# When VectorE reads a product that TensorE makes behind two heads' convolutions: its steps ordered behind the masks, and one product of routed weights placed behind shared unit 1

## The chip, the cores and the metric

The kernel runs on one core of a Trainium2 chip. A core has five engines with a queue of instructions each: TensorE (PE, matrix products; its weight loads are listed as PEld), VectorE (DVE), ScalarE (ACT), GpSimdE (POOL) and SyncE (SP), which mostly starts DMAs. They meet through semaphores: an instruction at the head of its queue waits until what it needs has been signalled, and everything behind it on the same engine waits too. The metric is the device time of one execution in microseconds (us).

## The reference: what is computed

`x` has 128 sequences of 32 heads (rows) with 512 positions each. Cut to what matters here:

```
K[h, l]   = 2 Re sum_n Ct[h,n] exp(dtA[h,n] l)              # a kernel of 512 taps per head
y[b,h]    = (causal convolution of x[b,h] with K[h] + D[h] x[b,h]) * (l < length[b])
scores    = sigmoid(y @ gate_w.T) + bias                    # 4096 rows y[b,h], 16 experts
the 4 best experts of each row, their scores scaled to sum 1
out       = x + sum over the 4 experts of w * ((silu(y Wg) * (y Wu)) Wd)
              + (silu(y Sg) * (y Su)) Sd                    # an expert that all rows share
```

All matrix products that carry y are in float32.

## The kernel before, in words

The work has three stages, and TensorE's order in each is written by hand.

**Convolutions.** The heads are done one at a time for heads 0 and 1 and then in pairs: (2,3), (4,5) up to (30,31). `convolve` (L593) multiplies the transposed input `xt` with `strip`, a 128 x 512 tile per head in which row p is the head's kernel shifted by p, into two PSUM tiles `py0` and `py1` (L599). VectorE then multiplies each with the mask `within` of the sequence lengths and writes `yb` (L617, "the mask"). One pair uses both PSUM tiles, so the next pair can only overwrite each once its mask is done. After the convolutions of a pair, `behind_head` (L943) puts other products in TensorE's order, first for the even head and then for the odd one: `turn_y` (L619, product L623) transposes the masked head before, which ScalarE copies to `yT` (L624); `gates` (L635, product L644) and `sums` (L658, product L661) make the gate's products into `parts` and `pg`; `kernels` (L379, product L407) makes the kernels of further heads into `pk`; the generator `ranks` (L502) sorts the sequences by length in small products (`by_rank_ps` L513, `k_u_ps` L533, `row_ps` L552); `weights_out` (L719, product L724) brings the chosen weights back to the order of rows.

The kernels of heads are made in six chunks of 4 to 8 heads. VectorE, ScalarE and GpSimdE make a chunk's exponentials and angles (`waves`, L303, held behind an earlier chunk's last step by `behind`), then the factors `gg_r`, `gg_i` (L398 to L403); TensorE multiplies them into `pk`; VectorE adds the skip term (`krow`, L415); SyncE writes the rows to memory (L422) and reads them back as `strip` (L433), one strip of 1 MB per four heads, in two buffers. Chunks 1 to 5 have their product behind heads 0, 3, 8, 14 and 20.

`route` (L669) chooses the experts of eight heads. It begins on VectorE with L683, which reads `pg`, and goes on through some 35 steps of 128 columns (a sigmoid in exp_parts L262 to L278, eight maxima L691, scans) to the weights `cw` (L716).

TensorE's order is fixed. VectorE's is not: the framework's scheduler sorts its instructions by the times that it assumes for them, and VectorE then executes them strictly in that order. The pairs of masks, the steps of the waves, and the steps that read `pk`, `by_rank_ps`, `k_u_ps`, `row_ps` and `pg` stand in one queue.

**Shared units.** Eight units of 512 rows go through the shared expert (`up` L1046, product L1052; `down` L1062, product L1067) in `unit_step` (L1094). Between them the generator `slots` (L737) makes the lists of routed tiles. `route` of the last eight heads stands behind the first quarter of unit 0, and two products of routed weights, of head blocks 2 and 3, behind unit 0:

```
        if u == 0:
            weights_out(NB // RB - 2)
            weights_out(NB // RB - 1)
```

**Routed tiles.** 134 tiles of 128 rows are gathered (L1017), transposed (L1147), multiplied with their expert's weights (L1179, L1205), and added to the output in memory (L1215).

Of the kernel before, what the change touches and what calls it, by code (L numbers as in the profile page):

```python
# [33 lines left out]
ALU = mybir.AluOpType  # L34
# [5 lines left out]
B, H, L, N = 128, 32, 512, 64  # L40
E, TOPK, I = 16, 4, 256
# [38 lines left out]
def ssm_moe_kernel(  # L80
# [15 lines left out]
    nc = tc.nc  # L96
# [61 lines left out]
    def dep(of, on, why):  # L158
        tc.add_manual_dep(of.ins, on.ins.name, SYNC, reason=why)
# [296 lines left out]

    chunk_last = {0: chunk0}

    def behind(op, c0=CHUNKS[2][0]):


        own = [c for c, _ in CHUNKS].index(c0)
        dep(op, chunk_last[CHUNKS[own - 1 if own > 2 else 0][0]], "later in VectorE's order")
# [38 lines left out]
    def ranks():  # L502

        to_rank_h = const.tile([P, P], F16, tag="to_rank_h", name="to_rank_h")
        last_chunk = chunk_last[max(chunk_last)]

        def later(op):
            dep(op, last_chunk, "later in VectorE's order")

        later(nc.vector.tensor_copy(to_rank_h, to_rank))  # L510

        by_rank_ps = ps_m.tile([P, 2], F32, tag="m", name="by_rank_ps")
        nc.tensor.matmul(by_rank_ps, lhsT=to_rank_h, rhs=num_len, start=True, stop=True)  # L513
        by_rank = const.tile([P, 2], F32, tag="by_rank", name="by_rank")
        nc.vector.tensor_copy(by_rank, by_rank_ps)
        yield


        reach = const.tile([P, KT], BF16, tag="reach", name="reach")
        later(nc.vector.memset(reach, 1.0))  # L520
        for n in range(1, KT):
            nc.vector.tensor_scalar(
                reach[:, n : n + 1], by_rank[:, 1:2], float(n * P), None, ALU.is_gt
            )

        unit = const.tile([P, NU], BF16, tag="unit", name="unit")
        later(nc.vector.tensor_scalar(unit, upos, 0.0, None, ALU.is_equal))
        reach_sum = const.tile([P, 1], F32, tag="reach_sum", name="reach_sum")
        nc.vector.tensor_reduce(reach_sum, reach, AX.X, ALU.add)
        reach_b = const.tile([P, 1], BF16, tag="reach_b", name="reach_b")  # L530
        nc.vector.tensor_copy(reach_b, reach_sum)
        k_u_ps = ps_m.tile([1, NU], F32, tag="m", name="k_u_ps")
        nc.tensor.matmul(k_u_ps, lhsT=reach_b, rhs=unit, start=True, stop=True)  # L533
        yield
        k_u = const.tile([1, NU], I32, tag="k_u", name="k_u")
        nc.vector.tensor_copy(k_u, k_u_ps)


        div = const.tile([P, 2], F32, tag="div", name="div")
        mod = const.tile([P, 1], F32, tag="mod", name="mod")  # L540
        later(floor_div(div[:, 0:1], rank, UB))
        later(floor_div(div[:, 1:2], ppos, UB))
        nc.vector.scalar_tensor_tensor(mod, div[:, 0:1], -float(UB), rank, ALU.mult, ALU.add)
        same_mod = const.tile([P, P], F16, tag="same_mod", name="same_mod")
        nc.vector.tensor_scalar(same_mod, pmod, mod, None, ALU.is_equal)
        row_u = const.tile([P, NU], F16, tag="row_u", name="row_u")
        nc.vector.tensor_scalar(
            row_u, cpos[:, :NU], div[:, 0:1], ppos, ALU.is_equal, ALU.mult
        )
        yield  # L550
        row_ps = ps_m.tile([P, NU], F32, tag="m", name="row_ps")
        nc.tensor.matmul(row_ps, lhsT=same_mod, rhs=row_u, start=True, stop=True)  # L552
        part = const.tile([P, TU // P], F32, tag="part", name="part")
        nc.vector.tensor_scalar(
            part, cpos[:, : TU // P], float(P // UB), div[:, 1:2], ALU.mult, ALU.add
        )
        unit_rows = const.tile([P, NU, TU // P], I32, tag="unit_rows", name="unit_rows")
        nc.vector.scalar_tensor_tensor(
            unit_rows,
            row_ps.unsqueeze(2).to_broadcast([P, NU, TU // P]),  # L560
            float(H),
            part.unsqueeze(1).to_broadcast([P, NU, TU // P]),
            ALU.mult,
            ALU.add,
        )
        of_ranks.update(by_rank=by_rank, reach=reach, k_u=k_u, unit_rows=unit_rows)


# [6 lines left out]
    within = const.tile([P, L], F32, tag="within", name="within")  # L575
# [14 lines left out]
    pys = [ps_g.tile([P, L], F32, tag="g", name=f"py{i}") for i in range(2)]  # L590
    skip = {}

    def convolve(tb, qs, xt, yb):  # L593
        def products(n):
            c0 = n * TS
            for q in qs:
                for jt in range(KT):

                    nc.tensor.matmul(  # L599
                        pys[q % 2][:, c0 : L - jt * P],  # L600
                        lhsT=xt[:, jt, q, :],
                        rhs=strip[tb][:, q, jt * P + c0 :],
                        start=(jt == 0),
                        stop=(jt == KT - 1 or L - (jt + 1) * P <= c0),
                    )
                    if L - (jt + 1) * P <= c0:
                        break

        if len(qs) == 1:
            products(0)  # L610
        else:

            if not skip:
                skip[0] = nc.tensor.value_load(skips[0:1, 0:1], min_val=0, max_val=SKIPS - 1)
            by_number(skip[0], 0, SKIPS - 1, products)
        for q in qs:
            nc.vector.tensor_mul(yb[:, q, :L], pys[q % 2], within)  # L617

    def turn_y(h, yb):  # L619
        q = h % HB  # L620
# [12 lines left out]
    pgs, cws, by_head, parts_last = {}, {}, {}, []  # L633
# [35 lines left out]
    def route(rb):  # L669
        nh = RB * HB  # L670
        hs = slice(rb * nh, (rb + 1) * nh)

        def stile(name, shape=(nh, E)):
            return sp.tile([P, *shape], F32, tag=name, name=f"{name}{rb}")

        def flat(t):
            return t.rearrange("p h e -> p (h e)")

        def over_e(t):
            return t.to_broadcast([P, nh, E])  # L680

        s, neg = stile("s"), stile("neg", (nh * E,))
        nc.vector.tensor_scalar(neg, pgs[rb][:, : nh * E], -1.0, None, ALU.mult)  # L683
        exp_into(neg, neg, f"sig{rb}", sp)
        nc.vector.tensor_scalar(neg, neg, 1.0, None, ALU.add)
        nc.vector.reciprocal(flat(s), neg)
        nc.vector.tensor_add(s, s, bias_b.unsqueeze(1).to_broadcast([P, nh, E]))

        top = stile("top", (nh, 8))
        for n in range(nh):  # L690
            nc.vector.max(top[:, n, :], s[:, n, :])  # L691
        last = top[:, :, TOPK - 1 : TOPK]
        above, same, nth, free = stile("above"), stile("same"), stile("nth"), stile("free", (nh, 1))
        nc.vector.tensor_tensor(above, s, over_e(last), ALU.is_gt)
        nc.vector.tensor_tensor(same, s, over_e(last), ALU.is_equal)
        heads_run = run_e[:, :nh, :]
        nc.vector.tensor_tensor_scan(
            flat(nth), flat(heads_run), flat(same), 0.0, ALU.mult, ALU.add
        )
        nc.vector.tensor_reduce(free[:, :, 0], above, AX.X, ALU.add)  # L700
        nc.vector.tensor_scalar(free, free, -1.0, float(TOPK), ALU.mult, ALU.add)
        nc.vector.tensor_tensor(nth, nth, over_e(free), ALU.is_le)
        nc.vector.tensor_mul(same, same, nth)
        nc.vector.tensor_add(above, above, same)
        nc.vector.tensor_copy(sel[:, :, hs].rearrange("p e h -> p h e"), above)
        nc.vector.tensor_tensor_scan(
            flat(nth), flat(heads_run), flat(above), 0.0, ALU.mult, ALU.add
        )
        nc.vector.tensor_mul(choice[:, hs, :], nth, above)
        nc.vector.tensor_mul(s, s, above)  # L710
        tot = stile("tot", (nh, 1))
        nc.vector.tensor_reduce(tot[:, :, 0], s, AX.X, ALU.add)
        nc.vector.tensor_scalar(tot, tot, 1e-20, None, ALU.add)
        nc.vector.reciprocal(free, tot)
        cw = stile("cw")
        nc.vector.tensor_mul(cw, s, over_e(free))  # L716
        cws[rb] = cw
# [225 lines left out]
    def behind_head(h):  # L943
# [4 lines left out]
        if h in kernels_at:  # L948
            c = kernels_at[h]
            chunk_last[c[0]] = kernels(*c, *made_waves[c])  # L950

        if strips[-1] in (tb, tb + 1) and strips[-1] < NB and strips[-1] * HB in kd_of:
            kernel_strip(strips[-1])
# [140 lines left out]
    def unit_step(u):  # L1094
# [15 lines left out]
                    next(making, None)  # L1110
        if u == 0:
            weights_out(NB // RB - 2)
            weights_out(NB // RB - 1)
        for q in range(TU // P):
            if u > 0:
# [227 lines left out]
```

## Time and profile before

| | us |
|---|---|
| median of 3 runs | 930.07 (929.57 to 930.26) |
| the profiled execution | 929.21 |
| its span, first to last instruction | 927.5 |
| TensorE busy | 877.9 |
| VectorE busy | 413.8 |
| convolutions, 22.5 to 135.5 us of the span | 113.0, TensorE busy 99.2, VectorE 78.2 |
| shared units, 135.5 to 279 us | 143.5, TensorE busy 140.7 |
| routed tiles, 279 us to the end | 648.5, TensorE busy 632.0 |

Two views answer most questions about such a kernel. The list of waits says which line of an engine waited for which line of another, for how long in total, how often, and the longest. The timeline lists one engine's instructions in order: start and length in us, line, output and inputs, shape, and, in square brackets, idle time before it and what ended that. Float32 products are issued in two halves, so that eight records are one set of four products. PEclk is the clock granted to TensorE as a share of full speed.

### The profile page before, as it was taken

Reading aid. Unit: us, or ns where it says so; the run is one execution under the profiler, and the core shown is the slowest. Engines: PE = TensorE matmul, PEld = TensorE weight load, DVE = VectorE, ACT = ScalarE, POOL = GpSimd, SP = SyncE. Lnnn points to the kernel's source line nnn. Section 1 sums busy time; section 2 is a strip of 40 time slices with the busy share of each in tenths; the row PEclk is TensorE's granted clock in tenths of the full one; section 3 lists DMA queues with packets and bytes.
Section 4 is the critical chain, followed back from the end, with each engine's and each line's share of the span. In section 5 each row is a group of like instructions: output and inputs, shape, how many; then the busy total and the mean of one; then the engine's idle time right before and its main releaser. Section 6 shows DMA issues by size and latency. Waiting matters only on the chain. (4 is left out here: it accounts for less than half of the span.)

```text
span 927.5 us, 14675 instructions
## 1 busy us (share of the span) xinstructions
PE 877.9 (95%) x2976; PEld 447.9 (48%) x2976; DVE 413.8 (45%) x1488; ACT 189.5 (20%) x379; POOL 420.7 (45%) x372
## 2 busy tenths in 40 slices
PE   2878899999999999999999999999999999999994
PEld 1656664444444444444444444444444444544441
DVE  8857655677841233423343334333433233343332
ACT  1221221111222112212221122211221112122211
POOL 1210010223456455645564556545655545556554
PEclk9998999999999999999999999999999999999998
DMA  5675659496869766776678567756766556677575
GB/s 204 198 232 173 222 175 333 56 317 120 151 153 206 163 115 118 141 174 105 115 137 187 102 111 136 127 103 110 132 113 114 102 100 109 114 126 138 106 127 102
DMA packets 54710, 136.03 MB, mean 147 GB/s; under 512 B 12432, under 2 KB 12592, under 8 KB 50992
## 3 DMA queue, kind: packets, MB, share of 16 engines
q0 software_dynamic: 36256, 89.77, 53.3%
q1 hardware_dynamic: 14096, 36.15, 11.4%
q10 hardware_dynamic: 4224, 8.39, 2.4%
q8 instruction: 76, 1.25, 0.5%
q14 instruction: 58, 0.48, 0.2%
HBM read 288.08 MB, written 60.64 MB: 376 GB/s over the span
## 5 line engine op out<-in xcount | busy, mean ns | idle before, releaser
L1179 PE MATMUL g<-store,yt 128*128 x742 | 343.1, 596 | 2.1 <-issue 1.3
L1215 POOL DMA_INDIRECT out<-ob,put x134 | 212.2, 1584 | 234.5 <-DVE junk L1154 189.8
L1205 PE MATMUL o<-store,zT 128*128 x536 | 252.0, 592 | 0.0
L1191 DVE SCALAR_TENSOR_TENSOR zt<-g,wt,sgt 128x256 f32<-128x256 f32 x135 | 65.3, 484 | 306.5 <-ACT sgt L1190 297.5
L1179 PEld LDWEIGHTS g<-store,yt 128*128 128x128 f32 x742 | 130.3, 190 | 119.1 <-issue 118.2
L1205 PEld LDWEIGHTS o<-store,zT 128*128 128x128 f32 x536 | 101.5, 190 | 128.6 <-issue 124.4
L1017 POOL DMA_INDIRECT yg<-y_rows,get x140 | 138.5, 989 | 49.6 <-issue 29.2
L1214 DVE COPY ob<-o 128x512 f32<-128x512 f32 x134 | 92.7, 692 | 109.1 <-PE o L1205 103.4
L1153 ACT COPY yt<-m 128x512 f32<-128x512 f32 x136 | 79.7, 586 | 224.9 <-PE m L1147 221.3
L1190 ACT ACTIVATE sgt<-g 128x256 f32<-128x256 f32 x135 | 51.9, 384 | 269.7 <-PE g L1179 231.5
L1076 POOL DMA_INDIRECT out<-ob,unit_rows x32 | 50.2, 1568 | 94.3 <-ACT ob L1074 88.3
L1147 PEld LDWEIGHTS m<-ident,yg 128*128 128x128 f32 x373 | 48.7, 141 | 72.3 <-issue 71.8
L599 PE MATMUL py<-strip,xt 128*128 128x192 f32 (+7 forms) x256 | 67.6, 419 | 0.0
L1147 PE MATMUL m<-ident,yg 128*128 128x128 f32 x373 | 63.0, 273 | 0.6 <-issue 0.6
L1067 PE MATMUL o<-store,z 128*128 128x512 f32 x128 | 57.7, 597 | 1.1 <-ACT yt L1153 1.1
L1200 DVE COPY zT<-u 128x256 f32<-128x256 f32 x134 | 56.3, 420 | 0.4 <-PE u L1197 0.4
L599 PEld LDWEIGHTS py<-strip,xt 128*128 128x128 f32 x256 | 46.3, 203 | 20.6 <-issue 15.4
L1197 PE MATMUL u<-ident,zt 128*128 128x128 f32 x268 | 51.2, 273 | 0.6 <-DVE zt L1191 0.6
L1052 PE MATMUL g<-store 128*128 128x512 f32 x92 | 43.0, 602 | 1.8 <-issue 0.9
L1052 PE MATMUL u<-store 128*128 128x512 f32 x92 | 42.2, 593 | 0.0
L902 DVE TENSOR_SCALAR cols<-tpos_h,stl,tok 128x143 f16<-128x143 f16 x128 | 41.6, 329 | 0.0
L1067 PEld LDWEIGHTS o<-store,z 128*128 128x128 f32 x128 | 23.4, 190 | 26.8 <-issue 25.4
(285 smaller groups left out, 493.0 us busy)
## 6 DMA issues: line engine op xcount, KB each, us to landing
store<-in_w_all SPq DMA_DIRECT2D x143, 1536.0 KB
xt<-in_x_t SPq DMA_DIRECT2D x8, 1024.0 KB
y_rows<-yb ACTq DMA_DIRECT2D x8, 1024.0 KB
out<-in_x POOLq DMA_DIRECT2D x8, 1024.0 KB
strip<-kd SPq DMA_DIRECT2D x7, 1024.0 KB
yg<-y_rows,get POOLq DMA_INDIRECT x140
out<-ob,put POOLq DMA_INDIRECT x134
strip<-kd SPq DMA_DIRECT2D x4, 256.0 KB
```

The lines of the kernel that those rows point to most:

```text
L599: nc.tensor.matmul(pys[q % 2][:, c0 : L - jt * P], lhsT=xt[:, jt, q, :], rhs=strip[tb][:, q, jt * P + c0 :], start=(jt == 0), stop=(jt == ...
L1017: nc.gpsimd.indirect_dma_start(out=at(yg, t), out_offset=None, in_=y_rows[:, :], in_offset=bass.IndirectOffsetOnAxis(ap=made["get"][:, t : ...
L1052: nc.tensor.matmul(ps[it], lhsT=w_sh[:, c0 : c0 + P], rhs=yT[:, u, kt, :, :].rearrange("p h b -> p (h b)"), start=(kt == KT - n), stop=(kt ...
L1067: nc.tensor.matmul(po, lhsT=at(zu, u)[:, it, q * P : (q + 1) * P], rhs=w_sh[:, c0 : c0 + L], start=(it == 0), stop=(it == IT - 1),)
L1147: nc.tensor.transpose(pt[:, q, :], at(yg, t)[:, q * P : (q + 1) * P], ident)
L1153: nc.scalar.copy(at(yt, t), pt)
L1179: mm = nc.tensor.matmul(pgu, lhsT=at(yt, t)[:, q, :], rhs=ring_flat[:, bass.ds(w0s[t] + q * 2 * I, 2 * I)], start=(q == KT - n), stop=(q = ...
L1191: nc.vector.scalar_tensor_tensor(at(zs, t), pgu[:, I:], at(wts, t), sg, ALU.mult, ALU.mult)
L1200: nc.vector.tensor_copy(at(zts, t), at(p_z, t))
L1205: mm = nc.tensor.matmul(po, lhsT=at(zts, t)[:, it, :], rhs=ring_flat[:, bass.ds(w0s[t] + WD + it * L, L)], start=(it == 0), stop=(it == IT ...
L1214: nc.vector.tensor_copy(ob, po)
L1215: add = nc.gpsimd.indirect_dma_start(out=out, out_offset=bass.IndirectOffsetOnAxis(ap=made["put"][:, t : t + 1], axis=0), in_=ob, in_offse ...
```

## The change

A list `masks` collects every mask that is issued, and `behind_masks` makes an instruction depend on the latest one. Since masks and the other steps are on the same engine, the dependency needs no semaphore: it fixes their order in VectorE's queue. It is put on the steps that read a product which TensorE makes behind a pair: `by_rank`, `k_u`, `unit_rows`, the first step of `route`, and the last step of `kernels` (`krow`). The product of the last block's weights moves from behind unit 0 to behind the products of unit 1.

```diff
+    masks = []
+
+    def behind_masks(op):
+        dep(op, masks[-1], "later in VectorE's order")
...
-        nc.vector.tensor_copy(by_rank, by_rank_ps)
+        behind_masks(nc.vector.tensor_copy(by_rank, by_rank_ps))
...
-        nc.vector.tensor_copy(k_u, k_u_ps)
+        behind_masks(nc.vector.tensor_copy(k_u, k_u_ps))
...
-        nc.vector.scalar_tensor_tensor(
+        rows = nc.vector.scalar_tensor_tensor(
             unit_rows,
...
+        behind_masks(rows)
...
-            nc.vector.tensor_mul(yb[:, q, :L], pys[q % 2], within)
+            masks.append(nc.vector.tensor_mul(yb[:, q, :L], pys[q % 2], within))
...
-        nc.vector.tensor_scalar(neg, pgs[rb][:, : nh * E], -1.0, None, ALU.mult)
+        behind_masks(nc.vector.tensor_scalar(neg, pgs[rb][:, : nh * E], -1.0, None, ALU.mult))
...
             chunk_last[c[0]] = kernels(*c, *made_waves[c])
+            behind_masks(chunk_last[c[0]])
...
         if u == 0:
             weights_out(NB // RB - 2)
+        if u == 1:
             weights_out(NB // RB - 1)
```

## The prediction

> **What bounds the kernel now.** The page first: TensorE is busy 95% of the span, yet in the slices of the convolutions (23.2 us each) it falls to 7 and 8 tenths, and only there its clock falls too.
>
> ```profile
> PE   2878899999999999999999999999999999999994
> DVE  8857655677841233423343334333433233343332
> PEclk9998999999999999999999999999999999999998
> ```
>
> Then the waits, TensorE's and VectorE's, from 20 to 140 us:
>
> ```profile
> PE pt L623 <- DVE yb L617: 11.5, 5, 3.1
> PE pk L407 <- DVE gg_r L400: 1.3, 1, 1.3
> ...
> DVE krow L415 <- PE pk L407: 8.9, 2, 5.4
> ...
> DVE neg L683 <- PE pg L661: 5.6, 3, 2.4
> DVE krow L415 <- PE k_u_ps L533: 4.6, 1, 4.6
> DVE by_rank L515 <- PE by_rank_ps L513: 3.2, 1, 3.2
> ```
>
> TensorE waits for the mask of a pair's even head, and VectorE waits for small products that stand behind that pair. The timeline shows one as the cause of the other. TensorE:
>
> ```profile
> 47.09 3.87 PE L599 MATMUL py<-strip,xt 128*128 128x448 f32 x16
> ...
> 51.51 0.66 PE L623 MATMUL pt<-to_rank,yb 128*128 128x128 f32 x4
> 55.23 1.08 PE L623 MATMUL pt<-to_rank,yb 128*128 128x128 f32 x4 [3.06 <-DVE yb L617]
> ```
>
> VectorE:
>
> ```profile
> 51.62 0.28 DVE L415 TENSOR_TENSOR krow<-pk,dsk 32x128 f32<-32x128 f32 x1 [5.35 <-PE pk L407]
> ...
> 54.41 0.68 DVE L617 TENSOR_TENSOR yb<-py,within 128x512 f32<-128x512 f32 x1
> ```
>
> Pair (8,9) starts at 47.09. Undisturbed pairs (115.80 to 118.59 and 119.63) let their masks start 2.8 and 3.8 us after the pair, so head 8's could have run at 49.9. It runs at 54.41, behind `krow` and nine wave steps. Windows of 3.41 us then give the clock:
>
> ```profile
> 54.67:58.08 3.41, 2.85 (x7) 1.92 (x8) 3.41 (x16) 1.27 (x3) 0.00 (x0) 0.50 0.96 298
> 71.74:75.15 3.41, 3.41 (x9) 2.38 (x8) 1.13 (x7) 0.35 (x1) 0.00 (x0) 0.50 0.03 10
> ```
>
> The third number from the end is the granted clock: 0.50 behind this gap and behind the one at 70.84; 81.98 to 85.39 and 102.46 to 105.87 read 0.50 too.
>
> **What goes away.** The gaps ahead of L623 are 0.68 (pair 4,5), 3.06 (8,9), 2.97 (12,13), 2.05 (14,15) and 2.71 (20,21): 11.5 us. The four half-clock stretches cost half of their part outside the gap: (3.41-0.56)/2 + 3.41/2 + 3.41/2 + (3.41-0.32)/2 = 6.4. Together 17.9, if nothing new is late.
>
> [...] The row: each of the four gaps is followed by exactly 3.41 us at 0.50, and the gaps of 1.34 (at 26.27) and 0.68 by none. I follow the row: a gap of about 2 us suffices, and its threshold is between 1.34 and 2.05.
>
> **What is late next.** In the built program's order of VectorE both masks of a pair now precede every step named. From the neg of block 0 (L683, behind pair 10,11) to the mask of head 16 this order has no slack, so I add up it and TensorE side by side, at full clock.
>
> TensorE: pair (6,7) starts 0.81 earlier, at 39.63: `krow` of chunk 2 moves 0.6 back behind a mask, but head 4's mask now ends by 38.9, before L623 is ready. Then 6.65 per long pair (115.80 to 122.48 is 6.68, 40.44 to 47.09 6.65), 4.58 per short one (111.22 to 115.80), plus 0.62 for sixteen `pk` records (50.89 to 51.51) or 0.37 for eight. (8,9) 46.28, (10,11) 51.5, (12,13) 58.2, `pg` ready 58.4 (63.74-63.55 = 0.19 later).
>
> VectorE from 58.4, starts to starts:
> - To head 12's mask: neg, ten sigmoid steps and four kernel steps, 2.75 in the trace (63.74 to 64.62, 68.01 to 70.01 without two `reach` steps); three more sigmoid steps 0.6, two wave steps 0.54, wm 0.27, two f_r 0.48; 0.35 since GpSimdE runs beside L394 and L398 (0.45 instead of 0.28 at 42.72). 5.0.
> - To head 14's: mask 0.6, six steps 0.8, mask 0.6, reciprocal 0.95, `by_rank`, bias, `reach` 0.45, maxima 0.63, five route steps 1.0. 5.0.
> - To head 15's: mask 0.6, route and `reach` steps 0.9. 1.5.
> - To `krow` of chunk 4: mask 0.6, sel 0.14, scan 0.33, three steps 0.58. 1.65.
> - To head 16's: route's last four steps and wr 1.05; the wave of 96 columns with seven `ranks` steps between, 0.12 and 0.17 apart, 3.9; from wm to the mask 2.35, as 90.45 to 92.39 and gg_i, which now stands ahead. 7.3.
> Sum 20.45, and the mask's own 0.68: head 16 is masked at 79.5.
>
> TensorE would be at its transpose, without waiting, at 58.2 + 4.6 + 7.3 + 4.3 = 74.4. So about 5.1 us of new waits: ahead of head 12's transpose (62.6 to 64.1) 1.5, of `k_u_ps`, whose `reach_b` is ready at about 69.8, 0.7, of head 16's 2.6 or more. Head 16's alone sets the time, since the chain runs on while TensorE waits. The last exceeds 2.05, so one half clock of up to 1.7 is likely behind it; the 1.5 lies between the known ends, and costs nothing, as VectorE sets the next point anyway.
>
> From there (18,19) 80.1 (was 88.56), (20,21) +6.68, (22,23) +4.95, (24,25) +6.65 = 98.4 (was 111.22): 12.8 earlier. Route of block 1 starts at 87.0, reaches head 20's mask 2.9 later, when that is just ready, and `krow` of chunk 5 waits behind both; no gap. Less the half clock, about 1.5: 11.3.
>
> **Queues and transfers moved.** `krow` delays SP's L422 and L433. Strip 3, wanted at 58.2: `krow` at 50.9, L433 1.9 later, 4.8 to land (53.63 until traffic ends in the slice 58 to 59), 57.7. Half a microsecond spare, and a miss is absorbed by head 12's wait. Strip 5: `krow` 71.5, L433 by 73.5, wanted at 86.8. ScalarE's y_rows issue now stands ahead of by_head for tb 3 and waits for head 15's mask at 70.7; parts are not ready before that. GpSimdE's waves wait for `krow` as before.
>
> **The moved weights product.** TensorE shows 152.35 with 0.86 waiting for `cw`, and 153.39 with 0.58 waiting behind it. From 151.11 to 153.39 is 2.28; without the second product 0.4 to 0.9 (its record 0.38, registers and branches up to 0.5). It costs 0.2 to 0.4 again at 167.7, where `cw` is 15 us old. Net 1.0 to 1.7, I take 1.3, as `cw`'s wait and a product measure it. ScalarE's copy there stands behind the second Silu of unit 1 and ahead of `ob`, which waits for a product of 3.6 us. Its 64 KB DMA on SP goes some 15 us later; the first gather that reads the columns is near 260, the first expert load behind it on SP at 186.
>
> After this TensorE has 632.0 of 648.5 us of work, and every transfer there is started by a step that moves along, so the gain arrives at the end.
>
> **Sum.** 929.21 (span 927.5 and 1.7 around it) - 11.3 - 1.3 = 916.6. The median stands 0.86 above the profiled time: 917.5.
>
> **Rivals.**
> [...]
> 2. The chain is up to a microsecond shorter, or the last wait falls across two windows, and no half clock comes: 930.07 - 12.8 - 1.3 = 916.0, with 1 less wait 915.0.
> 3. The waits only change places: 929 to 930.5. Against: the chain must be 13 us longer.
> 4. Slower: strip 5 comes late, because its `krow` stands behind head 15's mask and route's steps. TensorE holds pair (20,21), and all behind it, us for us. It lands 5 to 10 us after issue in the trace (61.34, traffic until 72): 78 to 84. It decides from about 101 on, when the 14 us are spent. That is 27 us for 1 MB.
>
> **How the numbers follow.** Forecast 0.67, range of its own 915.5 to 919.5; rival 2 0.13; rival 1 0.12; rival 3 0.04; rival 4 0.04. To leave out 2 in 10 at most: 915 to 921. A measurement tells 0.2% (1.9 us) from no change: faster 0.93, same 0.03, slower 0.04.
>
> **What would show it.** Right: no wait of TensorE for L617 at pairs (4,5), (8,9), (14,15), (20,21); remaining ones at heads 12 and 16, the latter largest; 0.50 at most once or twice between 50 and 110 us; pair (24,25) near 98 to 100; DVE's waits for `pk` short; L724's second product without wait. Wrong: L599 waiting for a strip, waits of over 4 us for head 16, three or more half clocks, or a stage of routed tiles longer than 648.5.

## The result, and the profile after

The changed kernel takes 916.39 us (median of 4 runs, 915.71 to 918.66); the kernel before took 930.03 beside it (929.57 to 930.26). The ratio is 0.986, with an interval of 0.984 to 0.988. The forecast was 917.5, from a sum of 916.6 for the profiled execution. That execution took 916.38, with a span of 914.7 against 927.5.

The page of the changed kernel, busy tenths in 40 slices of 22.9 us:

```profile
PE   2998999999999999999999999999999999999994
DVE  8986674967812334423343334333433333344332
PEclk9999999999999999999999999999999999999998
```

Of TensorE's 8, 7, 8, 8 in the slices of the convolutions one 8 is left, in the slice from 68.6 to 91.5 us, and the clock's 8 there is gone. The stage lies between 23.3 and 124.45 us now, with the same margins to the first convolution and to shared unit 0 as before: 101.15 us with TensorE busy for 94.3, where it was 113.0 us with 99.2. It is 11.9 us shorter, counted from a first convolution that starts 0.8 us later than before (23.36 and 22.54). The starts of a few products in the two timelines of TensorE show where the 12.8 us of span came from:

| first product of | before, us | after, us | earlier by |
|---|---|---|---|
| pair (4,5) | 34.92 | 35.52 | -0.60 |
| pair (8,9) | 47.09 | 46.90 | 0.19 |
| pair (12,13) | 63.55 | 58.81 | 4.74 |
| pair (16,17) | 82.50 | 74.46 | 8.04 |
| pair (18,19) | 88.56 | 81.71 | 6.85 |
| pair (24,25) | 111.22 | 100.34 | 10.88 |
| shared unit 0 | 136.39 | 125.34 | 11.05 |
| shared unit 1 | 153.39 | 140.28 | 13.11 |
| `down` of the shared units | 167.71 | 154.83 | 12.88 |

From the last row on next to nothing changes: the routed tiles take 648.7 us, before 648.5.

The list of waits of the changed kernel from 20 to 140 us (total, times, longest):

```profile
DVE yb L625 <- PE py L607: 12.5, 10, 2.9
DVE neg L691 <- PE pg L669: 11.1, 4, 5.5
...
PE pt L631 <- DVE yb L625: 4.9, 3, 2.4
...
PE py L607 <- DMA strip<-kd: 0.2, 1, 0.2
```

TensorE's waits for masks fell from 11.5 to 4.9 us. VectorE now waits for convolutions (L607) and for `pg`; no `krow` waits for `pk` in this list any more. Line 617 of before is 625 now, 623 is 631, and 599 is 607.

TensorE's timeline of the changed kernel at the pair shown before, at head 12 and at head 16:

```profile
46.90 3.87 PE L607 MATMUL py<-strip,xt 128*128 128x448 f32 x16
...
51.31 1.09 PE L631 MATMUL pt<-to_rank,yb 128*128 128x128 f32 x8
52.24 3.79 PE L607 MATMUL py<-strip,xt 128*128 128x448 f32 x16
...
65.27 0.63 PE L631 MATMUL pt<-to_rank,yb 128*128 128x128 f32 x4 [2.13 <-DVE yb L625]
65.74 5.52 PE L607 MATMUL py<-strip,xt 128*128 128x448 f32 x16
...
81.25 0.63 PE L631 MATMUL pt<-to_rank,yb 128*128 128x128 f32 x4 [2.42 <-DVE yb L625]
```

Behind pair (8,9) both transposes run as one group of 1.09 us, where 3.06 us of idle time parted them. Waits of 2.13 and 2.42 us are left, ahead of the transposes of heads 12 and 16 (and 0.32 behind pair (2,3)). The pair behind the first takes 5.52 instead of 3.87 us: the half clock, once. VectorE's timeline of the same stretch:

```profile
50.80 0.69 DVE L625 TENSOR_TENSOR yb<-py,within 128x512 f32<-128x512 f32 x1 [0.34 <-PE py L607]
...
51.58 0.28 DVE L415 TENSOR_TENSOR krow<-pk,dsk 32x128 f32<-32x128 f32 x1
...
58.89 0.29 DVE L691 TENSOR_SCALAR neg<-pg 128x128 f32<-128x128 f32 x1 [0.85 <-PE pg L669]
...
62.22 0.48 DVE L269 SCALAR_TENSOR_TENSOR sig_q<-sig_q,neg 128x128 f32<-128x128 f32 x1
...
63.44 0.28 DVE L269 SCALAR_TENSOR_TENSOR sig_q<-sig_q,neg 128x128 f32<-128x128 f32 x1
...
64.45 0.68 DVE L625 TENSOR_TENSOR yb<-py,within 128x512 f32<-128x512 f32 x1
...
70.26 0.69 DVE L625 TENSOR_TENSOR yb<-py,within 128x512 f32<-128x512 f32 x1 [0.70 <-PE py L607]
...
73.37 0.27 DVE L415 TENSOR_TENSOR krow<-pk,dsk 32x128 f32<-32x128 f32 x1
...
80.42 1.28 DVE L625 TENSOR_TENSOR yb<-py,within 128x512 f32<-128x512 f32 x2
```

`krow` (51.58) stands behind the mask (50.80), and neither is late. From `neg` at 58.89 to the masks of heads 16 and 17 at 80.42 VectorE is the engine that sets the time.

The window view with the clock (window, length, then busy time of PE, PEld, DVE, ACT and POOL, then the granted clock, third from the end):

```profile
63.26:66.67 3.41, 1.40 (x7) 1.04 (x8) 3.41 (x17) 1.09 (x2) 0.00 (x0) 1.00 1.02 397
66.67:70.08 3.41, 3.41 (x10) 2.20 (x9) 2.87 (x20) 0.00 (x0) 0.00 (x0) 0.50 0.04 15
76.91:80.32 3.41, 1.92 (x13) 1.33 (x11) 2.84 (x15) 1.04 (x2) 1.46 (x5) 1.00 0.64 225
80.32:83.74 3.42, 2.49 (x13) 1.97 (x14) 1.57 (x4) 0.58 (x1) 0.00 (x0) 1.00 0.16 31
```

One window at 0.50 between 20 and 140 us, where before had four. Head 12's wait of 2.13 us is followed by it, and head 16's longer one of 2.42 is not.

### The profile page after: what moved, and what is told of

Same layout as the page of the kernel before. It is cut to its first block, busy times and chain, and to the rows that moved or that the text cites. A ratio compares the mean times of both kernels' runs of the same rounds, so it can differ in the third digit from the quotient of the medians.

```text
span 914.7 us, 14680 instructions
## 1 busy us (share of the span) xinstructions
PE 873.1 (95%) x2976; PEld 445.6 (49%) x2976; DVE 415.0 (45%) x1488; ACT 188.8 (21%) x379; POOL 420.3 (46%) x372
## 3 DMA queue, kind: packets, MB, share of 16 engines
q8 instruction: 76, 1.25, 0.5%
## 4 chain that ended last, share of the span: by engine, by line
PE 67%; SPq 2%; issue 1%; POOL 0%; DVE 0%; ACT 0%; POOLq 0%; ACTq 0%
PE g L1189 34%; PE o L1215 24%; PE m L1157 4%; PE u L1207 3%; PE o L1076 1%; SPq L1240 1%; SPq L1294 0%; SPq L1276 0%; SPq L1275 0%; SPq L1277 0%; POOL out L1225 0%; SPq L1012 0%; DVE zt L1201 0%; ACT sgt L1200 0%; POOLq L1294 0%
## 5 line engine op out<-in xcount | busy, mean ns | idle before, releaser
L607 PE MATMUL py<-strip,xt 128*128 128x192 f32 (+7 forms) x256 | 64.0, 404 | 0.2 <-DMA strip<-kd 0.2
L607 PEld LDWEIGHTS py<-strip,xt 128*128 128x128 f32 x256 | 44.4, 195 | 19.0 <-issue 13.4
```

The source lines that it names most:

```text
L607: nc.tensor.matmul(pys[q % 2][:, c0 : L - jt * P], lhsT=xt[:, jt, q, :], rhs=strip[tb][:, q, jt * P + c0 :], start=(jt == 0), stop=(jt == ...
```

## Experiments

The theory: (a) steps at the head of VectorE's queue that wait for a product, `krow` above all, held the masks back, and this made the 11.5 us of gaps; (b) the gaps made the half clocks; (c) VectorE's own work from block 0's `neg` to head 16's mask is the next bound; (d) the moved product is a separate, small gain. The main rival to (b) is that the half clocks have another cause and stay when the gaps are filled; to (a), that the order hardly matters and waits change places.

| kernel | median, us (range) | ratio to before (interval) |
|---|---|---|
| only the order behind the masks | 919.75 (917.89 to 920.36) | 0.9878 (0.9860 to 0.9897) |
| only the weights product | 928.50 (926.86 to 930.40) | 0.9982 (0.9973 to 0.9990) |
| changed kernel, `krow` not behind masks | 922.87 (922.61 to 925.07) | 0.9927 (0.9906 to 0.9948) |
| before, products in four gaps | 922.98 (922.53 to 923.72) | 0.9921 (0.9902 to 0.9941) |
| changed kernel, only `krow` behind masks | 916.94 (915.68 to 918.14) | 0.9863 (0.9837 to 0.9888) |
| changed kernel, products in two gaps | 915.98 (914.92 to 917.84) | 0.9851 (0.9825 to 0.9877) |
| changed kernel, `ranks` four heads later | 912.82 (912.40 to 914.24) | 0.9820 (0.9797 to 0.9843) |
| the same, two chunks' `f_r` held back too | 913.68 (912.69 to 917.67) | 0.9839 (0.9807 to 0.9870) |

The kernel before took 930.0 beside the first four and 930.03 beside the others.

### The two halves of the change

Only the order (both products of routed weights behind unit 0 again):

```diff
         if u == 0:
             weights_out(NB // RB - 2)
-        if u == 1:
             weights_out(NB // RB - 1)
```

> The masks' order alone, both weights products behind unit 0 as before. My theory: the trace of after gains 11.05 us up to the first product of unit 0 and 1.8 around the weights product, so the 1.8 come back: 918.2 (917.4 to 919.0), with TensorE waiting again about 0.9 and 0.6 us at and behind the second product. Rival, the weights product was hidden anyway: 916.4.

Measured: 919.75, 1.5 us above the expected 918.2 and outside its range. Three quarters of the gain are in the order (10.3 of 13.6 us). Two lists of the profiled execution show what differs from the changed kernel: the waits from 20 to 140 us, and the windows around heads 12 and 16.

```profile
PE pt L631 <- DVE yb L625: 4.6, 3, 2.4
PE py L607 <- DMA strip<-kd: 1.8, 4, 0.9
```

```profile
64.22:67.64 3.42, 1.92 (x9) 1.40 (x10) 3.42 (x14) 0.80 (x2) 0.00 (x0) 1.00 0.90 348
77.88:81.29 3.41, 0.99 (x10) 0.76 (x8) 2.87 (x10) 0.58 (x1) 1.46 (x5) 1.00 0.05 15
81.29:84.70 3.41, 3.41 (x10) 2.19 (x8) 0.23 (x2) 0.58 (x1) 0.00 (x0) 0.50 0.90 244
```

Strips came late for 1.8 us in place of 0.2, the longest time 0.94 us ahead of pair (8,9). And here the half clock stands behind head 16, where the pair takes 5.47 in place of 3.83 us and nothing absorbs it, with the same wait of 2.42 us there as in the changed kernel. VectorE's order is the same in both kernels up to here. So the likely reading is that strips and half clocks fall differently from execution to execution; with one trace of each kernel this is not shown, but the five runs, from 917.89 to 920.36, leave room for it.

Only the weights product (the list `masks` and all its uses taken out):

```diff
-            masks.append(nc.vector.tensor_mul(yb[:, q, :L], pys[q % 2], within))
+            nc.vector.tensor_mul(yb[:, q, :L], pys[q % 2], within)
...
-            behind_masks(chunk_last[c[0]])
```

> The kernel before with the last weights product moved behind unit 1, masks as before. My theory: 928.2 (927.4 to 929.0), all four half clocks and the gaps of 2 to 3 us in the convolutions stay. Rival, hidden anyway or paid back by the ends of the gates: 930.0.

Measured: 928.50, as expected. The gaps are there as before (0.68, 3.06, 2.97, 2.04, 2.71), and the half clocks too: 0.50 at 56.71, 84.02 and 104.50 us, and from 70.36 on over two windows. What the move saves is read in TensorE's timeline. Before:

```profile
152.35 0.46 PE L724 MATMUL cw_ps<-cw,to_row 128*128 128x128 f32 x2 [0.86 <-DVE cw L716]
...
153.39 3.69 PE L1052 MATMUL g<-store 128*128 128x512 f32 x8 [0.58 <-ACT cw_o L728]
```

The changed kernel:

```profile
140.06 0.38 PE L732 MATMUL cw_ps<-cw,to_row 128*128 128x128 f32 x2
140.28 3.60 PE L1061 MATMUL g<-store 128*128 128x512 f32 x8
...
154.50 0.49 PE L732 MATMUL cw_ps<-cw,to_row 128*128 128x128 f32 x2
154.83 1.45 PE L1076 MATMUL o<-store,z 128*128 128x512 f32 x3
```

From unit 0's first product to unit 1's it is 17.00 us before (153.39 - 136.39) and 14.94 after, in the kernel with only this move as well (138.20 to 153.14), so 2.06 gained. The product costs 0.33 at its new place (154.83 - 154.50). Net 1.73; the times give 1.5.

### Which of the ordered steps matters

All but `krow` (the last line of the change in `behind_head` taken out), and `krow` alone (the other four uses taken out):

```diff
             chunk_last[c[0]] = kernels(*c, *made_waves[c])
-            behind_masks(chunk_last[c[0]])
```

> After, with krow's order behind the masks taken away, all others kept. My theory: krow causes the gaps at pairs (8,9), (14,15), (20,21) and their half clocks, so these come back, each 2 to 3 us and up to 1.7 of clock; what stays gone is the gap at (12,13), made by by_rank, and the weights product: 923 to 926, three half clocks. Rival, the order of by_rank and neg makes most of the gain: 917 to 919.

```diff
-        behind_masks(nc.vector.tensor_copy(by_rank, by_rank_ps))
+        nc.vector.tensor_copy(by_rank, by_rank_ps)
...
-        behind_masks(nc.vector.tensor_scalar(neg, pgs[rb][:, : nh * E], -1.0, None, ALU.mult))
+        nc.vector.tensor_scalar(neg, pgs[rb][:, : nh * E], -1.0, None, ALU.mult)
```

> After, with only krow ordered behind the masks; by_rank, k_u, unit_rows and neg are free again. In VectorE's built order by_rank (waiting for a product behind pair (12,13)) stands ahead of head 12's mask again. My theory: the gaps at (8,9), (14,15) and (20,21) stay away, head 12's wait grows from 2.1 to about 3.3, head 16's mask stands ahead of the last wave steps and its wait shrinks by about 2: 915.5 to 918. Rival, by_rank's and neg's order carries a third or more of the gain: 920 or more.

Measured: 922.87 without `krow`, 916.94 with it alone, against 916.39 for all. So the one line for `krow` is enough for the order's gain, to within what these runs tell apart, which confirms (a) for `krow`. The four other steps are not without effect: without `krow`'s line they still gain 7.1 us together with the moved product, which has 1.5 to 1.7 of it. The two parts overlap, so their gains do not add up. Without `krow`'s line the gaps at heads 8 and 20 come back as they were, 3.06 and 2.71 us. Head 14's does not, against my expectation; TensorE waits elsewhere instead. TensorE's timeline of the kernel without `krow`'s line:

```profile
55.96 0.63 PE L631 MATMUL pt<-to_rank,yb 128*128 128x128 f32 x4 [3.06 <-DVE yb L625]
...
75.85 0.17 PE L540 MATMUL k_u_ps<-unit,reach_b 128*1 128x8 bf16 x1 [2.17 <-DVE reach_b L538]
```

Its windows at these two places:

```profile
53.66:57.07 3.41, 1.11 (x6) 0.91 (x7) 3.41 (x14) 0.45 (x1) 0.00 (x0) 1.00 0.46 124
57.07:60.48 3.41, 3.41 (x9) 2.27 (x8) 2.83 (x19) 0.85 (x3) 0.00 (x0) 0.50 0.50 184
74.14:77.55 3.41, 1.70 (x15) 0.87 (x16) 3.41 (x20) 0.51 (x2) 0.28 (x1) 1.00 0.58 173
77.55:80.96 3.41, 3.41 (x22) 2.69 (x21) 3.41 (x17) 1.07 (x3) 0.00 (x0) 1.00 0.92 311
```

Two half clocks (the other from 98.03 to 101.44 us), not the three I expected; a wait of 2.17 us gave none.

With `krow`'s line alone the four other steps stand where the scheduler puts them. Head 12's wait is 3.19 us then, and head 16's 0.19: the wait is moved along, and the time is the same as far as these runs tell.

### Do the gaps make the half clocks?

Eight bf16 products of 128 x 512 ahead of the transposes of heads 8, 12, 14 and 20, in the kernel before. Their outcome is overwritten by the transpose, and VectorE's order is that of before.

```diff
+    WARM_AT = {8: 8, 12: 8, 14: 8, 20: 8}
+
     def turn_y(h, yb):
...
+        for _ in range(WARM_AT.get(h, 0)):
+            nc.tensor.matmul(
+                pt,
+                lhsT=ones,
+                rhs=ones.unsqueeze(1).to_broadcast([P, KT, P]),
+                start=True,
+                stop=True,
+            )
```

> The kernel before with eight bf16 products of 128x512 (0.22 us each, 1.75 together) put into TensorE's order ahead of the transposes of heads 8, 12, 14 and 20, that is into its four gaps; they write the PSUM tile that the transposes write next, so the result is unchanged. Gaps and VectorE's order stay. My theory, that idle of about 2 us in a window halves the clock: no half clock, 923.6 (6.4 less than before), idle of 0.3 to 1.3 us left in each gap. [...]

Measured: 922.98. Its timeline of TensorE at head 8, and its window view from 20 to 140 us, where the kernel before reads 0.94 for the clock:

```profile
52.09 1.89 PE L625 MATMUL pt<-ones 128*128 128x512 bf16 x8
55.23 0.66 PE L633 MATMUL pt<-to_rank,yb 128*128 128x128 f32 x4 [1.25 <-DVE yb L617]
```

```profile
20.00:140.00 120.00, 113.24 (x640) 75.34 (x639) 84.74 (x343) 27.40 (x54) 14.64 (x37) 1.00 0.67 221
```

The mask comes no earlier: the transpose still starts at 55.23, as before. The products only fill part of the idle time: 1.25, 1.13, 0.23 and 0.89 us of it are left in the four gaps. The clock stays at full speed: 1.00 in this view and in one over 21.4 to 912 us as a whole, and no pair of convolutions takes more than 3.88 us. With the order untouched 7.0 us are gained in the medians, and shared unit 0 begins 6.12 us earlier in the trace (130.27 after 136.39). This settles (b): TensorE's idle time in the gaps, each under 3.1 us, made the half clocks, and the prediction's 6.4 us for them was right in size.

The same with five products ahead of head 12's transpose and six ahead of head 16's, in the changed kernel (`WARM_AT = {12: 5, 16: 6}`):

> After, with five bf16 products of 128x512 ahead of head 12's transposes and six ahead of head 16's, written where the transposes write next. My theory: idle of about 1.0 and 1.1 us is left, no half clock between 22 us and the end of the routed tiles; VectorE's chain sets head 16's mask, so only the 0.7 us that its mask of head 14 waited for the half-clocked pair come back: 915 to 916, and a smaller spread. Rival, the half clock of 3.41 us costs its full 1.7: 914.7 or less.

Measured: 915.98. There is no half clock up to the tail: no pair of convolutions takes more than 3.89 us, and the mean granted clock of the profiled execution is 0.996, where the changed kernel has 0.994. Idle of 0.44 and 1.03 us is left. The 0.4 us less than the changed kernel lie within the spread, and the runs alone would not exclude the rival. The traces are finer. From block 0's `neg` to head 16's mask it takes 20.73 us here (58.69 to 79.42), in the changed kernel 21.53 (58.89 to 80.42), and head 14's mask no longer waits 0.70 for its convolution. So the half clock behind head 12 costs 0.8 us at that point, about what was expected, and not its full 1.7. The kernel with only the order, which had no half clock there, took 20.73 too (59.32 to 80.05).

### Work taken out of VectorE's chain

If (c) holds, the steps of `ranks` between block 0's `neg` and head 16's mask set the time there, and their products are not needed so early. They go behind heads 17 to 20:

```diff
-        if 13 <= h <= 16:
+        if 17 <= h <= 20:
             next(rest_of_ranks, None)
```

> After, with the sorting of sequences placed behind heads 17 to 20 instead of 13 to 16, which takes its some twenty VectorE steps out of the stretch from neg of block 0 to head 16's mask. My theory, VectorE's in-order chain through that stretch sets the time: head 12's wait falls from 2.1 to about 0.7, head 16's from 2.4 to under 1, no half clock: 911 to 914. Rival, other waits (strips, the gate) take their place: 916.

Measured: 912.82, faster than both kernels. TensorE's waits for masks from 20 to 140 us, and two others:

```profile
PE pt L631 <- DVE yb L625: 1.7, 2, 1.4
...
PE by_rank_ps L520 <- DVE to_rank_h L517: 0.7, 1, 0.7
...
PE py L607 <- DMA strip<-kd: 0.4, 1, 0.4
```

Head 16's wait of 2.42 us is gone, head 12's is 1.39 (0.7 was expected), the half clock is gone (no pair of convolutions takes more than 3.89 us): 3.6 us for a change of two numbers. (c) holds.

What is left is head 12's wait. The kernel steps (L386 to L403) of the chunk whose product stands only behind head 14 precede head 12's mask in VectorE's order. I held its first steps, `f_r` (L386), behind head 13's mask, and those of the next chunk behind head 17's:

```diff
+    masks, kernel_first = [], {10: 13, 14: 17}
...
-            nc.vector.tensor_mul(f_r[rows, cs, j, :], cos[rows, :, LA:], mag[rows, :, LA:])
+            op = nc.vector.tensor_mul(
+                f_r[rows, cs, j, :], cos[rows, :, LA:], mag[rows, :, LA:]
+            )
+            if c0 in kernel_first:
+                dep(op, masks[kernel_first[c0]], "later in VectorE's order")
```

> As the kernel with the sorting behind heads 17 to 20, and the f_r steps of kernel chunks 4 and 5 ordered behind the masks of heads 13 and 17. My theory: head 12's wait goes wholly, 911 to 913. Rival as before: 916.

Measured: 913.68, a miss: the time is above the expected range, though these runs do not tell it from 912.82, and head 12's wait did not go but grew to 2.26 us. VectorE's timeline of this kernel ahead of head 12's mask:

```profile
61.14 0.29 DVE L405 TENSOR_TENSOR gg_r<-gg_r,gg_t 128x128 f32<-128x128 f32 x1 [0.96 <-POOL gg_t L404]
```

Only `f_r` moved. The steps behind it, `gg_r` among them, do not depend on `f_r`, and the scheduler now put them earlier, where VectorE stood 0.96 us for GpSimdE. A step held back makes room that the scheduler fills. Holding all of the chunk's steps was not tried.

## Why the prediction was right

**Total.** 916.6 was summed for the profiled execution, 916.38 measured. The 0.86 us that I added because the median stood so far above before's profiled run was not there: after's median is 0.01 above its own. Up to the first product of shared unit 0 the gain was 11.05 us (predicted 11.3), and from there to the first `down` product 1.8 (the weights product's 1.3). So small an error is partly luck: errors of up to 1.6 us cancel in it, and where the half clock falls alone is worth about that much. One reading of the page was too broad: the clock row has an 8 outside the convolutions too, in its last slice, before and after.

**What goes away.** The gaps at pairs (4,5), (8,9), (14,15) and (20,21) are gone, and three of the four half clocks. Products in the gaps gained 7.0 us from the kernel before, 6.1 of them in the trace up to shared unit 0; the sum had 6.4. Following the clock's row was right: filling gaps of 2.05 to 3.06 us ended the half clocks.

**The threshold was put in the wrong quantity.** I said that a gap of about 2 us suffices. The changed kernel refutes it as a length of gap: 2.13 gave a half clock and 2.42 none. The windows show what separates them. Head 12's gap lies almost whole in the window up to 66.67 and leaves 1.40 busy, 2.01 idle. Head 16's, 78.83 to 81.25, is cut at 80.32 into 1.49 and 0.92.

Over the profiles of six kernels (before, changed, only the order, only the weights product, without `krow`'s line, only `krow`'s), between 35 and 112 us, windows laid in steps of 3.413 us from an observed half clock give: 13 windows entered at full clock with 1.99 us or more idle, each followed by one at 0.50; and none with 1.71 or less followed by one. The nearest thing to a test is the kernel with only the order: with the same order of VectorE and the same wait of 2.42 us at head 16, its windows lie so that all of this wait falls into one (0.99 busy), and the half clock follows there. It is a pattern in all six profiles; no run moved the windows against a gap on purpose.

**Late next, the places.** The two waits stand at heads 12 and 16, the latter larger, as predicted (1.5 and 2.6 or more; 2.13 and 2.42 measured). The half clock was forecast behind head 16 and came behind head 12. `k_u_ps` was to wait 0.7 and did not, since the half clock made TensorE itself late for it. With that clock mended by products, it waited 0.70.

**Late next, the sizes.** The chain from `neg` to head 16's mask was summed as 20.45 us from start to start and took 21.53 (80.42 - 58.89):

| part, starts | predicted | measured |
|---|---|---|
| `neg` to head 12's mask | 5.0 | 5.56 |
| to head 14's mask | 5.0 | 5.81 |
| to head 15's | 1.5 | 1.46 |
| to `krow` of chunk 4 | 1.65 | 1.65 |
| to head 16's | 7.3 | 7.05 |

Where no half clock fell behind head 12 the chain took 20.73 us, 0.28 above the sum; the other 0.8 are the half clock's. The first part is the term that was too small. I gave 0.35 us to VectorE's running beside GpSimdE, and four sigmoid steps took 0.40 to 0.50 us instead of 0.22 to 0.28 there, 0.8 in all. The second holds 0.70 that head 14's mask waited for its convolution, which ran at half clock. Here the step "costs nothing, as VectorE sets the next point anyway" failed: that pair's end was itself the next point, by 0.70.

**The cancelling.** Pair (12,13) started 0.6 later than predicted, because TensorE was late from its first pairs on (pair (4,5): 35.52 in place of 34.92), and the chain took 1.08 longer. So pair (18,19) started at 81.71 and not at 80.1. In return the 1.5 us of half clock behind it did not come: that was luck, since the kernel with only the order had it just there. Pair (24,25) started at 100.34, where 98.4 plus 1.5 had been forecast.

**The weights product.** The gain at its old place was under-sized. Of the 2.28 us from 151.11 to 153.39 I had left 0.4 to 0.9 there; 0.22 are left (140.06 to 140.28), and 2.06 went. The 0.5 us for registers and branches in that was my estimate, which no run shows. At the new place 0.33 lies within the 0.2 to 0.4.

**Rivals.** The case without a half clock (915 to 916) was right in that none fell behind head 16, and its time was missed because the chain was longer, not shorter. Half clocks that stay (17.9 - 6.4 - 5.1 + 1.3 = 7.7 gained, 922.4) fell with the products in the gaps. Waits that only change places (929 to 930.5) fell with 4.9 us in place of 11.5. Strip 5, which had to decide the slower case, was never waited for at pair (20,21). Strip 3's half a microsecond spare was about right: pair (12,13) waited for it 0.20 to 0.47 us in three of the experiments, and not in the changed kernel. The prediction did not price the strip of pair (24,25): the changed kernel waits 0.20 us for it, and all five other kernels that have `krow`'s line 0.37 to 0.57.

## What to carry to other kernels

On an engine that executes in order, a step that waits for another engine's late product is paid by everything behind it (here TensorE stood 3.06 us at head 8 with `krow` ahead of the masks, and not at all with it behind them): look at what the waiting instruction stands in front of, and order the step that frees the bottleneck's buffer first. After that sum the engine's queue from point to point, since its own work sets the next bound (here 21.53 us from `neg` to head 16's mask); work there that nobody needs yet (`ranks`, 3.6 us) is the next gain. Short gaps of TensorE cost more than half as much again in clock as in idle time here (6.4 beside 11.5 us). As far as these profiles show, what counts is the idle time within one clock window (in windows entered at full clock, 1.99 us or more was followed by a half clock each time, 1.71 or less never), and not the length of the gap.

## What the runs showed of the hardware that was not expected

- The granted clock goes in windows of 3.413 us that do not start with the gap: the four half clocks of the kernel before begin at 54.67, 71.74, 81.98 and 102.46 us, that is 5, 3 and 6 such windows apart. Within one such window 1.99 us of idle time sufficed for a half clock. The narrowest case, the kernel with only the weights product:

```profile
80.60:84.02 3.42, 1.42 (x13) 1.45 (x14) 3.42 (x20) 1.17 (x3) 0.00 (x0) 1.00 0.60 187
84.02:87.43 3.41, 3.41 (x10) 2.21 (x9) 3.31 (x21) 0.55 (x2) 0.00 (x0) 0.50 0.93 279
```

- In that same kernel a window at half clock with 0.95 us idle was followed by a second one at half clock, 6.83 us together; with 0.58 or less idle it never was.
- VectorE's sigmoid steps of 128 columns slowed at head 12 while GpSimdE multiplied: in the timeline above the same step took 0.48 us at 62.22 and 0.28 at 63.44. GpSimdE's timeline of the changed kernel ends its products between the two:

```profile
62.09 0.47 POOL L399 TENSOR_TENSOR gg_t<-ge_i,ct_i 128x128 f32<-128x128 f32 x1
62.64 0.53 POOL L402 TENSOR_TENSOR ge_i<-ge_i,ct_r 128x128 f32<-128x128 f32 x1
```

  The kernel with `ranks` four heads later has such steps too: three from 60.49 to 61.70 took 0.42 to 0.54 us, and from 62.24 on they took 0.28. With `f_r` held back as well the sigmoid step L266 took 0.49 us at 61.35, beside a product of GpSimdE (0.51 us from 61.18), and 0.28 at 61.89, behind it. Not every step slows (in the changed kernel L398 takes 0.28 at 62.63, beside GpSimdE's product of 62.64), and what decides it, the operands or which engine starts first, was not tried.
- With the same order of VectorE, the strip of pair (8,9) came 0.94 us late in the profiled execution of the kernel with only the order, and in time in that of the changed kernel. TensorE's waits from 20 to 140 us hold no strip in any of the four kernels without `krow`'s line, which wait 4.2 to 11.5 us for masks.
